# Sharing PSUM banks between two halves of a four-layer vision kernel, and walking its last stage backwards

## The chip, the core and the metric

The kernel runs on one core of a Trainium2 chip. The metric is the device time of one execution in microseconds. Times are the median of several executions; a profile is taken of one further execution, by the hardware profiler.

## The reference

Four layers run one after the other on `x`, eight images of 64 channels by 64 x 64 pixels, in fp32. Cut to what matters here:

```python
# layer 0: attention over all 4096 pixels of an image, depthwise 3x3, 1x1
v = relu(bn(einsum('bchw,oc->bohw', x, w1)))
prob = softmax(einsum('bdn,bdm->bnm', Q, Q) / sqrt(64))        # Q = x as (b, 64, 4096)
out = bn(conv1x1(relu(bn(dwconv3x3(einsum('bnm,bdm->bdn', prob, V)))))) + x
# layer 1: two Swin blocks (8x8 windows, 8 heads, the second shifted by 4)
for i in range(2):
    t = t + window_attention(layernorm(t))
    t = t + gelu(layernorm(t) @ f1w + f1b) @ f2w + f2b
# layer 2: 3x3 filter with weights made from the data, leaky relu, 1x9 convolution, residual
# layer 3: selective scan in four directions, then SAFM
xi, z = split(layernorm(x) @ in_proj)                          # 128 channels each
xc = silu(dwconv3x3(xi))
for k in range(4):                                             # rows, columns, both reversed
    dts, Bs, Cs = split(xproj[k] @ xs[k])
    dt = softplus(dtproj[k] @ dts + dtproj_b)
    h = h * exp(dt * A) + dt * Bs * xs                         # 16 states, along 4096 pixels
    y += sum_over_states(h * Cs) + D * xs
x = x + (layernorm(y) * silu(z)) @ outproj
n = channel_layernorm(x)
out = x + gelu(aggr @ concat(dwconv of 4 groups, pooled by 1, 2, 4, 8, brought back up)) * n
```

## The kernel before

**Tiling.** Two images stand on the 128 partitions at a time, 64 channels each, so the batch is four pairs p = 0 to 3. A pair's 4096 pixels are worked in eight columns of 512 pixels (`CH` and `TD`, one PSUM bank of fp32 each). All of it is in the class `_Direct`. A second, general path at the end of the program runs only when the data are out of range; with these inputs it does not run.

**Stages.** For each pair there are three: `front(p)` (layers 0, 1, 2, and `scan_sources`, which makes xc, its transposed copy and z for the scans and writes them to memory), `scans(p)` and `back(p)`. The front and the back are generators that yield after each piece of work with a number that says how much it was. `tile_kernel` runs `front(0)` alone; then four times `scans(p)`, each with the list `back(p-1)`, `front(p+1)` beside it; then `back(3)` alone. Inside `scans`, after each of its steps, `next(beside, cost)` is drawn until the share of the work done matches the share of the steps gone, over all but the last 24 (`LEAD`). The cost of a back is put at 0.25 of that of a front. Beside the last scans there is only `back(2)`, and with this estimate it is used up about half way, at step 257 of 512; from then on `done >= cost`, and the rest of the last scans runs alone.

**The scans.** A pair has 64 units: two images, four directions, eight chunks of 512 pixels. A unit has eight steps with two of the 16 states each, so 512 steps. `inputs` (L1643 and on) prepares the next unit: SP loads `xs`; PE makes the bank `pdd` (L1655); ACT applies Exp and Ln (L1657, L1660); DVE multiplies into `du` (L1661); PE makes the bank `pbc` (L1664) and ACT copies it to `bc`, which SP writes out as `rows`. A step then takes: SP's two fetches of B and C, each spread over all partitions (L1675); POOL's product `vd` = B x du (L1680); for each of two states ACT's `dad` = exp(du x A) into a bank (L1700), DVE's scan along the 512 pixels (L1703) and ACT's copy of the last value into `carry` (L1711); then the product with C, on POOL for both states (L1714), or, in odd steps and throughout the last pair, one on POOL (L1716) and one on DVE (L1717); and PE adds both products with an identity matrix into the bank `yd` (L1730). At the end of a unit DVE adds `yd` to `Y` (L1741 and around), and in the fourth direction SP writes the sum out as `ys`, which the back reads.

**The front, where banks are used.** `normed` (L1199) is a norm over channels: PE `pc` (L1201, centred values), ACT `n_sq` (L1203), PE `pv` (L1205), ACT `n_sd` by Ln and Exp (L1207, L1208); it leaves `pc` in its bank until DVE has used it. Window attention goes through eight rows of eight windows: scores into `w_s` (PE L1393), bias on DVE (L1405), Exp on ACT (L1410), weighing into `w_av` (PE L1420), division on DVE (L1436), transposing into `w_ot` (PE L1444), and projection into `w_pp`. The multi-layer perceptron (MLP), column by column: `normed`, two `ph` (PE L1485), two Gelus on ACT (L1487), `pf` (PE L1492), and its sum on DVE. `scan_sources`: eight columns of `normed`; then per image eight `pi` (PE) with ACT's copies into the padded tile `XI` (L1570), the 3x3 convolution on DVE over nine taps a column (`xacc`, L1217 and L1221), Silu on ACT (L1577), and eight `pz` with Silu and a write to memory.

**The back.** The first loop takes the columns from 0 to 7. Per column there are three norms: for either image `yb` and `zb` are loaded, `normed` gives `pc` and `pv`, DVE makes `u` (L1765, L1766) and PE multiplies into `po` (L1767); then DVE adds into `X` (L1769), and a third `normed` and DVE write the padded tile `F` (L1772). Then come three pooling levels (L1785 and on), then eight columns of the closing part: nine taps of `sacc` on DVE (L1217, L1221), ACT's copy `S` (L1808), PE `pa` (L1810, L1814), Gelu, and two operations of DVE (L1822 to L1825) before the write.

**Banks.** All eight PSUM banks are given out by two pools. `ps_scan` has three with the tag "da" (`dad`, `pdd`, `pbc`) and one with the tag "y" (`yd`). `ps_front` has three with the tag "f", which all of `bank()` comes from (L1178), and one with the tag "acc", which `total()` gives (`po` of layer 0, `w_av`). A tag's banks go round: the next tile takes the one used longest ago and waits until that one's last reader is done.

**Order.** The instructions are issued in the order of the program, and a scheduler of the framework then sets each engine's order with the waits that buffers and data need. It decides again whenever a pool or a loop changes, so an edit to a pool can move instructions that are not named in it. On the chip the order is fixed.

Of the kernel before, what the change touches and what calls it, by code (L numbers as in the profile page):

```python
# [9 lines left out]
F32 = mybir.dt.float32  # L10
# [5 lines left out]
B, C, HH, WW = 8, 64, 64, 64  # L16
L = HH * WW
P = 128
CH = 512
NCH = L // CH  # L20
# [4 lines left out]
TD = 512  # L25
# [200 lines left out]
class _Net:  # L226
    def __init__(self, ctx, tc, x, packs, layout, out):
        self.tc, self.nc = tc, tc.nc
        self.x, self.out = x, out
        nc = self.nc  # L230
        self.const = ctx.enter_context(tc.tile_pool(name="const", bufs=1))
        self.dram = ctx.enter_context(tc.tile_pool(name="rows", bufs=2, space=bass.MemoryType.DRAM))
        self.packs, self.layout, self.w = packs, layout, {}
        self.load(self.const, (0, 1))
        with tc.tile_pool(name="temp", bufs=1) as temp:
            self.load(temp, (2,))
            self.prepare()
# [910 lines left out]
class _Direct:  # L1148
# [8 lines left out]
    def __init__(self, net, ctx):  # L1157
        self.net, self.tc, self.nc, self.w = net, net.tc, net.nc, net.w
        tc = self.tc
        self.dram = ctx.enter_context(tc.tile_pool(name="mem", bufs=2, space=bass.MemoryType.DRAM))  # L1160
        one = ctx.enter_context(tc.tile_pool(name="scan1", bufs=1))
        self.Y = one.tile([P, L], F32, name="Y", tag="Y")
        self.carries = one.tile([P, NST], F32, name="carry", tag="carry")
        self.sw = ctx.enter_context(tc.tile_pool(name="scan", bufs=2))
        self.slabs = ctx.enter_context(tc.tile_pool(name="slabs", bufs=3))
        self.ps = ctx.enter_context(tc.tile_pool(name="ps_scan", bufs=3, space=PSUM))
        self.pf = ctx.enter_context(tc.tile_pool(name="ps_front", bufs=3, space=PSUM))
        self.kept = {}

    def padded(self, name):  # L1170
        t = self.slabs.tile([P, SLAB], F32, name=name, tag="slab").rearrange("p (h w) -> p h w", w=66)
        self.net.pad_border(t, 66, self.nc.vector)
        return t
# [1 line left out]
    def flat(self, name):  # L1175
        return self.slabs.tile([P, SLAB], F32, name=name, tag="slab")[:, 0:L]

    def bank(self, name, shape=(P, CH)):  # L1178
        return self.pf.tile(list(shape), F32, name=name, tag="f")

    def total(self, name, shape=(P, CH)):
        return self.pf.tile(list(shape), F32, name=name, tag="acc", bufs=1)
# [431 lines left out]
    def scans(self, p, beside, cost):  # L1614

        self.units = []
        for im in range(2):
            out = self.memory("ys")  # L1620
            self.kept["y", 2 * p + im] = out
            for nth, k in enumerate((1, 3, 0, 2)):
                order = range(NTD) if k < 2 else range(NTD - 1, -1, -1)
                self.units += [dict(image=2 * p + im, k=k, c=c, at=at, nth=nth, out=out) for at, c in enumerate(order)]
        self.inputs(self.units[0])
        n = 8 * len(self.units)
        steps = [{} for _ in range(n)]
        done = 0
        for i in range(-3, n):
            if i + 3 < n:  # L1630
                self.fetch(i + 3, steps[i + 3], 0)
            if 0 <= i + 2 < n:
                self.fetch(i + 2, steps[i + 2], 1)
                self.products(i + 2, steps[i + 2])
            if i >= 0:
                self.step(i, steps[i])
                if i:
                    self.sums(i - 1, steps[i - 1], steps[i]["w"])
                while done < cost * (i + 1) / (n - LEAD):
                    done += next(beside, cost)  # L1640
            if i % 8 == 1 and i // 8 + 1 < len(self.units):
                self.inputs(self.units[i // 8 + 1])
        self.sums(n - 1, steps[n - 1])  # L1643
        self.run(beside)
# [37 lines left out]
    def step(self, i, st):  # L1682

        nc, w, net = self.nc, self.w, self.net
        wk, ps = self.sw, self.ps
        u = self.units[i // 8]
        k, c, at, CC, v = u["k"], u["c"], u["at"], st["C"], st["v"]

        n0, rp = 2 * (i % 8), i % 2 or u["image"] >= B - 2
        rev = k >= 2  # L1690

        def along(t):
            return t[:, ::-1] if rev else t

        h = wk.tile([P, 2 - i % 2, TD], F32, name="hd", tag=f"h{i % 2}", bufs=1)
        hs = []
        for j in range(2):
            n = n0 + j
            da = ps.tile([P, TD], F32, name="dad", tag="da")
            nc.scalar.activation(da, u["du"][:, 0], AF.Exp, scale=net.As[:, k, n : n + 1])  # L1700
            first = 0.0 if at == 0 else self.carries[:, n : n + 1]
            to = da if rp and j else h[:, j]
            nc.vector.tensor_tensor_scan(along(to), along(da), along(v[:, j]), first, ALU.mult, ALU.add)  # L1703
            hs.append(to)
            if at < NTD - 1 and (rp or j):
                ends = h[:, :, 0] if rev else h[:, :, TD - 1]
                cs = self.carries[:, n0 : n0 + 2]
                if rp:
                    ends = to[:, 0:1] if rev else to[:, TD - 1 : TD]
                    cs = self.carries[:, n : n + 1]  # L1710
                nc.scalar.activation(cs, ends, AF.Copy)  # L1711

        if rp == 0:
            st["w"] = nc.gpsimd.tensor_tensor(v, h, CC, ALU.mult)  # L1714
        else:
            st["w"] = nc.gpsimd.tensor_tensor(v[:, 0], h[:, 0], CC[:, 0], ALU.mult)  # L1716
            nc.vector.tensor_tensor(v[:, 1], hs[1], CC[:, 1], ALU.mult)  # L1717
# [30 lines left out]
    def back(self, p):  # L1748
# [2 lines left out]
        X = self.flat("X3")  # L1751
        F = self.padded("F")
        with tc.tile_pool(name="w4", bufs=2) as wk:
            for c in range(NCH):
                cols = slice(c * CH, (c + 1) * CH)
                nc.sync.dma_start(X[:, cols], self.kept["x", p][:, cols])
                po = self.bank("po3")
                for im in range(2):
                    y = wk.tile([P, CH], F32, name="yb", tag="yb")
                    z = wk.tile([P, CH], F32, name="zb", tag="zb")  # L1760
                    nc.sync.dma_start(y, self.kept["y", 2 * p + im][:, cols])
                    nc.sync.dma_start(z, self.kept[2 * p + im][2][:, cols])
                    pc, sd = self.normed(wk, lambda pc: [(pc, y)], w["cen128"], w["avg128"], net.eps[:, 0:1])
                    u = wk.tile([P, CH], F32, name="u", tag="u")
                    nc.vector.scalar_tensor_tensor(u, pc, w["on_g"], sd, ALU.mult, ALU.mult)  # L1765
                    nc.vector.scalar_tensor_tensor(u, u, w["on_b"], z, ALU.add, ALU.mult)  # L1766
                    nc.tensor.matmul(po[half[im]], lhsT=w["opT"], rhs=u, start=True, stop=True)  # L1767
                    yield 6
                nc.vector.scalar_tensor_tensor(X[:, cols], po, w["outproj_b"], X[:, cols], ALU.add, ALU.add)  # L1769
                pc, sd = self.normed(wk, lambda pc: [(pc, X[:, cols])], w["cen64"], w["avg64"], net.eps[:, 1:2])  # L1770
                d = self.rows(F, c)
                nc.vector.scalar_tensor_tensor(d, self.img(pc), w["cn_g"], self.img(sd), ALU.mult, ALU.mult)  # L1772
                nc.scalar.activation(d, d, AF.Identity, bias=w["cn_b"])
                yield 6
# [55 lines left out]
@with_exitstack  # L1830
def tile_kernel(ctx: ExitStack, tc: tile.TileContext, x: bass.AP, packs, layout, out: bass.AP):
    net = _Net(ctx, tc, x, packs, layout, out)
    with ExitStack() as path:
        net.open(path, True)
        d = _Direct(net, path)
        net.log_exp()
        front = d.run(d.front(0))
        back = 0.25 * front
        for p in range(B // 2):
            works, cost = [], 0  # L1840
            if p:
                works.append(d.back(p - 1))
                cost += back
            if p + 1 < B // 2:
                works.append(d.front(p + 1))
                cost += front
            d.scans(p, d.chain(*works), cost)
        d.run(d.back(B // 2 - 1))

    with tc.tile_pool(name="check", bufs=1) as pool:  # L1850
        bad = net.in_range(pool)
    with tc.If(bad > 0), ExitStack() as path:
        net.open(path, False)
        for p in range(B // 2):
            t = net.layer0(p)
            t = net.layer1(t)
            t = net.layer2(t)
            net.layer3(t, p)
# [21 lines left out]
```

## Time and profile before

| | |
|---|---|
| median of 3 runs | 14083.28 us (14071.26 to 14084.42) |
| the profiled execution, its own time | 14074.21 us |
| its span, first to last instruction | 14072.3 us |
| mean granted clock of TensorE | 0.865 |

The page's first part gives each engine's busy time over the span; the groups give the costliest kinds of instructions (busy time and mean duration, then idle time just before them and what ended most of it):

```profile
PE 11340.1 (81%) x46358; PEld 4189.8 (30%) x46358; DVE 8432.1 (60%) x9763; ACT 7036.3 (50%) x15453; POOL 8173.2 (58%) x4111
...
L1680 POOL TENSOR_TENSOR vd<-B,du 128x1024 f32<-128x1024 f32 x2048 | 4842.5, 2369 | 3955.8 <-DVE xacc L1217 1888.8
L1730 PE MATMUL yd<-vd,pack 128*128 128x512 f32 x8192 | 4577.0, 686 | 1175.1 <-POOL vd L1714 419.8
L1703 DVE TENSOR_TENSOR_SCAN hd<-dad,carry,vd 128x512 f32<-128x512 f32 x2464 | 3092.6, 1270 | 1081.7 <-ACT dad L1700 681.2
...
L1716 POOL TENSOR_TENSOR vd<-hd,C 128x512 f32<-128x512 f32 x1280 | 1634.9, 1278 | 271.7 <-DVE hd L1703 244.6
```

The stages differ in what fills them. The windows of the trace give the busy time of each engine in each stage, here rounded to whole microseconds; the stage's borders are read from the timeline.

| stage (us from the span's start) | length | PE | DVE | ACT | POOL | clock |
|---|---|---|---|---|---|---|
| front 0: attention, 0 to 600 | 600 | 580 | 11 | 334 | 2 | 1.00 |
| depthwise and 1x1, to 670 | 70 | 23 | 65 | 12 | 0 | 0.57 |
| first norm, to 704 | 34 | 24 | 7 | 22 | 0 | 0.80 |
| window rows, block 0, to 985 | 281 | 238 | 72 | 91 | 0 | 0.61 |
| MLP, block 0, to 1070 | 85 | 57 | 11 | 43 | 0 | 0.60 |
| window rows, block 1, to 1355 | 285 | 241 | 83 | 92 | 0 | 0.64 |
| MLP, block 1, to 1452 | 97 | 64 | 13 | 51 | 0 | 0.62 |
| layer 2, to 1792 | 340 | 315 | 78 | 33 | 0 | 0.70 |
| scan sources and first inputs, to 1977 | 185 | 89 | 110 | 84 | 20 | 0.61 |
| scans of pairs 0 to 2 with their works, to 11650 | 9673 | 8139 | 6048 | 5173 | 6285 | 0.89 |
| last scans with back 2, to 12812 | 1162 | 770 | 1003 | 578 | 970 | 0.88 |
| last scans alone, to 13785 | 973 | 644 | 811 | 460 | 897 | 0.90 |
| last back, to 14072 | 287 | 156 | 119 | 65 | 0 | 0.61 |

A row is read against its length: an engine that is busy for nearly all of it sets the stage's time; where none is, the stage is a chain of dependent steps on several engines.

### The profile page before, as it was taken

To read this page: it belongs to the slowest core of one execution; us is meant where nothing else is said; L and a number is where in the kernel's file an instruction comes from. 1 tells how busy PE (TensorE), PEld (TensorE's weight loads), DVE (VectorE), ACT (ScalarE), POOL (GpSimd) and SP (SyncE) were. 2 spreads that over 40 slices of the span, in tenths; PEclk is the share of its full clock that TensorE was granted. 3 is DMA by queue.
4 is the path that set the end of the run, shared out by engine and by line. 5 is a ranking of instruction groups with operands and counts; after the bars stand their busy time and mean duration, and the time that the engine had idled before them with its cause. 6 is when DMAs were issued, how large, how long until landed. Compare 5 with 4: busy or idle time off the path is not lost. (4 is left out here: it accounts for less than half of the span.)

```text
span 14072.3 us, 141532 instructions
## 1 busy us (share of the span) xinstructions
PE 11340.1 (81%) x46358; PEld 4189.8 (30%) x46358; DVE 8432.1 (60%) x9763; ACT 7036.3 (50%) x15453; POOL 8173.2 (58%) x4111
## 2 busy tenths in 40 slices
PE   9888879979889668998889666998988866666665
PEld 2244222224433222223433222222443222222221
DVE  0222254467776875347675767336666677998884
ACT  5533145555553645555562644555554454454442
POOL 0000035677776765456674685456666678879991
PEclk9866679989889889998898788999888878988996
DMA  0000034456555764345553675345554577878882
GB/s 17 1 1 1 5 136 153 161 187 211 195 196 181 241 206 156 127 147 181 175 197 133 225 247 180 128 144 175 170 173 168 181 244 256 276 241 291 294 291 70
DMA packets 705498, 2379.22 MB, mean 169 GB/s; under 512 B 81060, under 2 KB 81188, under 8 KB 703980
## 3 DMA queue, kind: packets, MB, share of 16 engines
q1 hardware_dynamic: 681024, 2315.57, 48.5%
q10 hardware_dynamic: 23724, 54.50, 1.0%
q8 instruction: 367, 6.01, 0.2%
q14 instruction: 383, 3.14, 0.1%
HBM read 2269.08 MB, written 100.66 MB: 168 GB/s over the span
## 5 line engine op out<-in xcount | busy, mean ns | idle before, releaser
L1680 POOL TENSOR_TENSOR vd<-B,du 128x1024 f32<-128x1024 f32 x2048 | 4842.5, 2369 | 3955.8 <-DVE xacc L1217 1888.8
L1730 PE MATMUL yd<-vd,pack 128*128 128x512 f32 x8192 | 4577.0, 686 | 1175.1 <-POOL vd L1714 419.8
L1703 DVE TENSOR_TENSOR_SCAN hd<-dad,carry,vd 128x512 f32<-128x512 f32 x2464 | 3092.6, 1270 | 1081.7 <-ACT dad L1700 681.2
L1700 ACT ACTIVATE dad<-du,As 128x512 f32<-128x512 f32 x4096 | 2711.7, 679 | 985.0 <-DVE hd L1703 728.8
L1730 PEld LDWEIGHTS yd<-vd,pack 128*128 128x128 f32 x8192 | 1592.5, 212 | 3853.7 <-issue 1753.0
L1714 POOL TENSOR_TENSOR vd<-hd,C 128x1024 f32<-128x1024 f32 x768 | 1810.9, 2358 | 1365.4 <-DVE hd L1703 694.1
L1716 POOL TENSOR_TENSOR vd<-hd,C 128x512 f32<-128x512 f32 x1280 | 1634.9, 1278 | 271.7 <-DVE hd L1703 244.6
L1272 ACT ACTIVATE e<-s 128x512 f32<-128x512 f32 x2048 | 1199.2, 591 | 1030.0 <-PE s L1266 1028.1
L1703 DVE TENSOR_TENSOR_SCAN dad<-dad,carry,vd 128x512 f32<-128x512 f32 x1120 | 1426.0, 1273 | 62.7 <-ACT dad L1700 62.5
L1266 PE MATMUL s<-X 64*128 64x512 f32 x4096 | 1350.1, 646 | 114.1 <-ACT e L1272 113.8
L1258 PE MATMUL po<-e,VT 128*64 128x512 f32 x4096 | 1145.1, 629 | 17.0 <-ACT e L1272 17.0
L1711 ACT ACTIVATE carry<-hd 128x1 f32<-128x1 f32 (+1 forms) x1792 | 357.1, 201 | 1172.7 <-DVE hd L1703 1161.9
L1717 DVE TENSOR_TENSOR vd<-dad,C 128x512 f32<-128x512 f32 x1280 | 858.7, 671 | 82.1 <-ACT carry L1711 74.8
L1266 PEld LDWEIGHTS s<-X 64*128 64x128 f32 x4096 | 365.3, 186 | 1065.4 <-issue 820.8
L1420 PEld LDWEIGHTS w_av<-vals,w_e 64*64 64x64 f32 x16384 | 612.7, 159 | 178.0 <-ACT w_e L1410 69.9
L1420 PE MATMUL w_av<-vals,w_e 64*64 64x9 f32 x16384 | 638.5, 216 | 23.6 <-ACT w_e L1410 23.5
L1703 DVE TENSOR_TENSOR_SCAN hd<-dad,vd 128x512 f32<-128x512 f32 x352 | 420.2, 1210 | 203.0 <-ACT dad L1700 92.0
L1741 DVE TENSOR_TENSOR Y<-Y,yd 128x512 f32<-128x512 f32 x128 | 124.6, 973 | 656.0 <-PE yd L1730 655.7
L1410 ACT ACTIVATE w_e<-w_e 128x512 f32<-128x512 f32 x512 | 310.4, 627 | 382.2 <-DVE w_e L1405 254.9
L1655 PE MATMUL pdd<-xs,xdt 128*128 128x512 f32 x512 | 323.4, 718 | 204.3 <-DVE hd L1703 96.7
L1711 ACT ACTIVATE carry<-dad 128x1 f32<-128x1 f32 x1120 | 189.9, 170 | 589.1 <-DVE dad L1703 587.0
L1405 DVE TENSOR_TENSOR w_e<-w_s,bias 128x512 f32<-128x512 f32 x512 | 328.5, 682 | 248.4 <-PE w_s L1393 248.1
(247 smaller groups left out, 11078.1 us busy)
## 6 DMA issues: line engine op xcount, KB each, us to landing
B<-rows SPq DMA_DIRECT2D x2048, 512.0 KB, 5.0
C<-rows SPq DMA_DIRECT2D x2048, 512.0 KB, 4.5
xs<-xt SPq DMA_DIRECT2D x128, 256.0 KB, 2.9
xs<-xc SPq DMA_DIRECT2D x128, 256.0 KB, 3.1
xc<-xcv ACTq DMA_DIRECT2D x64, 256.0 KB, 4.3
zs<-z ACTq DMA_DIRECT2D x64, 256.0 KB, 3.9
xt<-XT ACTq DMA_DIRECT2D x32, 512.0 KB, 7.5
rows<-bc SPq DMA_DIRECT2D x256, 64.0 KB, 1.9
```

What stands on the lines that cost most here:

```text
L1258: nc.tensor.matmul(po[half[im]], lhsT=VT[:, t, half[im]], rhs=es[im], start=(t == 0), stop=(t == 31))
L1266: nc.tensor.matmul(ss[im], lhsT=at(half[im], t), rhs=X[half[im], jc * CH : (jc + 1) * CH], start=True, stop=True)
L1272: nc.scalar.activation(e, ss[im], AF.Exp, scale=C**-0.5, accum_out=parts[:, im, t, jc : jc + 1])
L1420: nc.tensor.matmul(self.av[half[im], x % 4 + j, h, :], lhsT=es[h // 4][half[im], j, h % 4, :], rhs=V[half[im], x + j, h, :], start=True, s ...
L1680: self.nc.gpsimd.tensor_tensor(v, st["B"], dx.to_broadcast([P, 2, TD]), ALU.mult)
L1700: nc.scalar.activation(da, u["du"][:, 0], AF.Exp, scale=net.As[:, k, n : n + 1])
L1703: nc.vector.tensor_tensor_scan(along(to), along(da), along(v[:, j]), first, ALU.mult, ALU.add)
L1711: nc.scalar.activation(cs, ends, AF.Copy)
L1714: st["w"] = nc.gpsimd.tensor_tensor(v, h, CC, ALU.mult)
L1716: st["w"] = nc.gpsimd.tensor_tensor(v[:, 0], h[:, 0], CC[:, 0], ALU.mult)
L1717: nc.vector.tensor_tensor(v[:, 1], hs[1], CC[:, 1], ALU.mult)
L1730: m = nc.tensor.matmul(y, lhsT=w["ident"], rhs=st["v"][:, j], start=(n == 0), stop=(n == NST - 1))
```

## The change

It has three parts. First, a counter `self.turn` is kept; while it is at or above zero, each call of `bank()` takes its tile from the tags "f" and "da" in turn, so that six banks go round instead of three. It is on during the whole of `front(0)`, off after it, and on again from the point in the last scans at which their beside work is used up, through to the end, so also in the last back. Second, the scans take `dad` by `bank()` with "da" as the default; while the counter is off that is the pool they had, and while it is on `dad` too alternates. `pdd` and `pbc` stay in "da" throughout, `yd` in "y". Third, the first loop of `back` goes through the columns from the last to the first, in all four backs; the closing loop keeps its order.

```diff
@@ __init__
+        self.turn = -1
@@ bank
-    def bank(self, name, shape=(P, CH)):
-        return self.pf.tile(list(shape), F32, name=name, tag="f")
+    def bank(self, name, shape=(P, CH), ours="f"):
+
+        if self.turn >= 0:
+            self.turn += 1
+            ours = ("f", "da")[self.turn % 2]
+        return (self.pf if ours == "f" else self.ps).tile(list(shape), F32, name=name, tag=ours)
@@ scans
                 if i:
                     self.sums(i - 1, steps[i - 1], steps[i]["w"])
+                if p == B // 2 - 1 and done >= cost:
+                    self.turn = max(self.turn, 0)
                 while done < cost * (i + 1) / (n - LEAD):
@@ step
-            da = ps.tile([P, TD], F32, name="dad", tag="da")
+            da = self.bank("dad", (P, TD), "da")
@@ back
-            for c in range(NCH):
+            for c in reversed(range(NCH)):
                 cols = slice(c * CH, (c + 1) * CH)
@@ tile_kernel
         net.log_exp()
+        d.turn = 0
         front = d.run(d.front(0))
+        d.turn = -1
         back = 0.25 * front
```

## The prediction

> **What bounds the kernel now.** I read the page first, then the busy time of the engines in short windows, then the timeline wherever a stage that the change touches begins, repeats or ends, and last the chain of waits. The change can act in three places: the first front, which runs alone; the second half of the last scans; the last back, which runs alone again. The scans between them keep their pools.
>
> ```profile
> span 14072.3 us, 141532 instructions
> ...
> PE   9888879979889668998889666998988866666665
> ...
> POOL 0000035677776765456674685456666678879991
> ```
>
> A slice is 352 us. PE's 9, 8, 8, 8, 8 over POOL's zeros are the first front (to about 1955 us), POOL's nines the last scans, its final 1 the last back. The windows say what holds each:
>
> ```profile
> 550.00:600.00 50.00, 50.00 (x194) 12.05 (x192) 0.69 (x1) 30.41 (x96) 0.00 (x0) 1.00 0.00 1
> 600.00:650.00 50.00, 17.98 (x139) 9.48 (x138) 47.23 (x70) 7.78 (x10) 0.00 (x0) 0.60 0.00 0
> 1000.00:1050.00 50.00, 34.27 (x57) 8.47 (x57) 6.02 (x9) 25.65 (x32) 0.00 (x0) 0.64 0.00 0
> 13400.00:13500.00 100.00, 64.76 (x123) 21.21 (x122) 87.78 (x90) 50.28 (x127) 97.58 (x56) 0.95 0.89 301
> ```
>
> The columns are PE, weight loads, DVE, ACT, POOL, granted clock, DMA share, GB/s. To 600 us PE is full: more banks give nothing. From 600 DVE is full with the convolution: nothing either. At 1000 (the MLP) nobody is full: a chain of PE, ACT and DVE. In the last scans POOL works 97 of 100 us. The timeline shows the chains, first one row of windows, then one MLP column:
>
> ```profile
> 732.75 1.03 PE L1444 MATMUL w_ot<-pack,w_o 128*64 128x128 f32 x4 [1.02 <-DVE w_o L1436]
> ...
> 736.18 2.07 PE L1205 MATMUL pv<-n_sq,pack 128*128 128x512 f32 x2 [0.69 <-ACT n_sq L1203]
> ```
> ```profile
> 1011.87 1.26 ACT L1487 ACTIVATE hid<-ph,bf 128x512 f32<-128x512 f32 x2 [0.76 <-PE ph L1485]
> 1012.61 2.55 PE L1492 MATMUL pf<-hid,pack 128*64 128x512 f32 x4 [0.74 <-ACT hid L1487]
> 1013.15 1.28 ACT L428 ACT_TABLE_LOAD   x1
> 1015.09 1.66 PE L1201 MATMUL pc<-X,pack 128*128 128x512 f32 x2
> ...
> 1017.43 1.12 PE L1205 MATMUL pv<-n_sq,pack 128*128 128x512 f32 x2 [0.69 <-ACT n_sq L1203]
> ```
> ```profile
> 1870.00 0.11 DVE L411 MEMSET XI<- 128x64 f32 x1
> 1897.37 0.69 DVE L1661 TENSOR_TENSOR du<-pdd,xs 128x512 f32<-128x512 f32 x1 [27.26 <-ACT pdd L1660]
> 1900.30 0.81 DVE L1221 TENSOR_SCALAR xacc<-XI,pack 128x512 f32<-128x512 f32 x1 [2.24 <-ACT XI L1570]
> ```
>
> The last fence is DVE idle for 30 us before the second image's convolution. For the end, the chain of waits gives the period of one column of the back, 13887.48 - 13863.49 = 24.0 us:
>
> ```profile
> 13863.49 2.02 PE pc L1201 x2
> 13866.18 2.09 PE pv L1205 x2
> ...
> 13887.48 2.02 PE pc L1201 x2
> ```
>
> **What the Trainium skill says.** "PSUM — Partial Sum Buffer", Specifications: eight banks of 512 fp32 values in each partition. The pools hold 3 + 1 and 3 + 1, all eight; so nothing is added, the change only lets one side use the other's three while that side rests. "TensorE: Matmul & The Clock Gate", Part 1: the clock is halved after about 3.4 us of idling and full after about that much steady work. The trace agrees: a pair of 128x512 passes takes 2.09 us in the chain above and 1.12 us at 1017. The same page, Architectural detail: ACT and DVE take their instructions strictly in order, so one placed early that is not ready holds all behind it; below, ACT's second XI waits 4.63 us for pi with pdd behind it. "ScalarE: Activation LUTs", What ACT_TABLE_LOAD costs: 1283 ns a load, and 1.28 us is what the trace has.
>
> **The change part by part.** The framework orders each engine's instructions anew, so I compared the built order of both programs. Outside the three places it differs only around the backs beside the scans; no compute instruction is added, and ACT gets 7 more table loads.
>
> First front. (a) Rows of windows: PE now takes half of the next scores before the first transpose, filling its 1.0 us wait for DVE, and the next row's pc inside the weighing, so that n_sq is done when pv comes: 0.69 us. 1.7 us x 15 rows = 25. (b) MLP: pc of the next column stands before pf. Before, pv came 1017.43 - 1011.87 = 5.6 us after the Gelus began (6.0 at half clock). After: pc 0 to 2.1, pf to 4.1 at half clock, while ACT does Gelus, load and n_sq by 1.26 + 1.28 + 0.60 = 3.2; pv at 3.3 to 4.1. Say 2.0 x 15 columns = 30. (c) First norm: it took 30 us for 8 columns; ACT needs 0.58 + 0.69 + 0.63 + 0.72 = 2.62 each, 21, so 8; the norm of the sources 3.05 to 2.62, 3; p_m ahead of the last pf, 2. (d) Second image: all eight pi now stand before the scans' pdd, which had held PE 7.05 us for a DMA and left ACT waiting 4.63 us for pi. ACT's first XI stays at 1885.3, its second comes at once, so the convolution starts near 1887, 13 earlier, and without two of the scans (1.2 each): 16. Sum 84. Bounds: 50 (the filled holes return half to PE's slower matmuls) and 110.
>
> The price of (d): the first scan's pdd moves behind that convolution; its wait is taken from the first steps. Behind it on ACT stand two xcv, then loads for Silu, Ln, Silu and Exp in turn (three loads more, 3.9 us). From the end of the convolution: xcv and XT 2.8, four DMA issues 3, z and load 2, Ln 0.6, z and two loads with its issue 3.6, du and bc 1.2, then 5.9 as before from bc to POOL's first product, 2 x 2.35 for two more: step 2's scan at about +26. Before, it began at 1977.2, 25.8 after the convolution. So zero, within 10 either way.
>
> Last scans, from step 257 of 512: the last 260 steps took 973 us, 3.74 each; POOL needs 2.373 + 1.275 = 3.65. The floor is thus 24 us away. More banks let dad run ahead at unit borders, where DVE sat 83 us over 23 borders waiting for du; but SP's fetches keep their place. I take 10; bounds 25 gained, and 15 lost.
>
> Backs beside the scans: reversed columns no longer wait for the last unit's ys (PE stood 58.6 us in 16 waits for yb, matmuls and weight loads together, the last back's included). Four loads more at half-busy ACT are hidden. I take 5, bounds 25 either way, since DVE is 90 to 99 per cent busy in the third of them and any bad order shows.
>
> Last back. Its early start does not come: in the built order a single pc (yb) is ahead of the last yd, and before, the first image's po was already done in the scans; the first column needs about 20 us against 21. Per column the order becomes pc pc pv po pv po pc pv. At half clock throughout: eight pairs 16.4 + gaps 3.0 + 3.0 + 0.92 + 0.67 + 0.6 (n_sq before Exp) = 24.6, no gain; if the second pc and first pv come at full clock, as five pairs now follow without a gap, 22.3. Between +4 and -12 for seven columns; I take -8. Reversal also puts the first four sacc taps behind the last column instead of in DVE's idle time: 4 x 0.75 = +3, memsets moved out -1; the closing columns, DVE 59 of 66 us busy, -3. Together -9.
>
> Sum: 84 + 10 + 5 + 9 = 108. The profiled execution took 14074.2 us (span 14072.3): 13966. The median, 14083.3, is 9 above that execution: 13975.
>
> **The rivals.** *The clock takes it back.* The front's windows already grant 0.6; if work put in the holes runs at half speed, (a) and (b) vanish, as do last scans and back: 29 + 5 remain, 14049. For: PE 43 of 50 us busy in the rows. Against: pc in the MLP replaces waiting, not matmuls. *A larger gain.* Denser rows lift the clock from about 0.62 to 0.8: of 560 us of rows some 400 hang on PE, a fifth is 80 to 90 more: 13888. For: the same matmuls take 1.12 us elsewhere; against: no row shows it. *Slower: the head of POOL's queue.* In the last half POOL's order moves in most units; if at each border a product waits for its B while a ready vd stands behind it, the steps fall to the 4.2 to 4.4 us of the half with the back beside it. At 0.55 more for 255 steps: +140 - 108, 14115. It decides from (108 + 28) / 255 = 0.53 us a step. For: POOL waited 29.5 us for B already there. Against: the pattern at a border, three products, one vd, two products, then vds, is the same in both orders. *The change does not do what it says*: for the reversal's head start this is so, and it is in the sum.
>
> **How the numbers follow.** A measurement here tells 0.2 per cent, 28 us, from no change. Forecast 0.62 (own range 13930 to 14030), clock 0.16, larger gain 0.14, slower 0.08. The range 13900 to 14052 holds the forecast, most of the clock case and part of the larger gain. Faster: 0.61 + 0.09 + 0.14 = 0.84; same 0.09; slower 0.07.
>
> **What would show it.** The second image's convolution ending near 1867 instead of 1951 us, and POOL's first product 19 later, near 1886 instead of 1904.87; the convolution's first xacc of image two within 3 us of the second XI; MLP columns near 8 to 10 us; rows near 33; steps of 3.65 to 3.75 in the last half; column period 22 to 24.6 at the end. The forecast is wrong if the front's end moves by less than 50 us, or if the last half takes more than 3.85 us a step.

## The result, and the profile after

| | before | changed |
|---|---|---|
| median, runs taken side by side | 14077.27 us (14064.28 to 14084.42) | 14018.69 us (14012.53 to 14040.87) |
| ratio, with its 95% interval | | 0.9962 (0.9945 to 0.998) |
| span of the profiled execution | 14072.3 us | 14010.7 us |

The kernel became faster, by 58.6 us; 108 were forecast. On the page of the changed kernel POOL's first slice of work, the sixth, has a 4 instead of a 3: the scans begin earlier.

```profile
span 14010.7 us, 141613 instructions
...
POOL 0000046578767765556665685457666688878982
```

The same four windows as before (PE, weight loads, DVE, ACT, POOL, granted clock, DMA share, GB/s) show where to look:

```profile
550.00:600.00 50.00, 49.76 (x234) 14.07 (x234) 3.60 (x10) 28.07 (x90) 0.00 (x0) 1.00 0.00 1
600.00:650.00 50.00, 17.30 (x92) 7.71 (x88) 48.69 (x75) 8.99 (x12) 0.00 (x0) 0.58 0.00 0
1000.00:1050.00 50.00, 35.79 (x207) 13.59 (x206) 10.74 (x15) 31.91 (x41) 0.00 (x0) 0.83 0.00 0
13400.00:13500.00 100.00, 62.55 (x113) 21.86 (x114) 83.12 (x87) 44.46 (x99) 93.99 (x54) 0.90 0.87 289
```

In the MLP at 1000 us ACT is busier and the clock is 0.83 where it was 0.64. In the last scans POOL, which had been busy for 97.58 of 100 us, is at 93.99. POOL is what those scans wait for, so they must have become slower. To say by how much, I took one event that all kernels have in the same number, the end of the addition of `yd` into `Y` at the end of each of the 256 units, and compared it between the two traces. Units are counted from 0 in each pair's scans, and the lead is the time by which the changed kernel is earlier:

| place | before | changed | lead |
|---|---|---|---|
| end of the second image's convolution | 1951.5 | 1863.9 | 87.6 |
| end of unit 1 of the first scans | 2064.5 | 1983.9 | 80.6 |
| end of the scans of pair 0 | 4981.1 | 4916.0 | 65.1 |
| pair 1 | 8338.9 | 8258.6 | 80.3 |
| pair 2 | 11691.4 | 11612.9 | 78.5 |
| unit 31 of the last scans | 12806.8 | 12720.2 | 86.6 |
| unit 63, the last | 13785.7 | 13760.3 | 25.4 |
| end of the span | 14072.3 | 14010.7 | 61.6 |

Three things happened. The front gained 88 us. The second half of the last scans lost 61 of them. The last back gained 36. In between, the lead wanders by up to 15 us, also over the scans of pair 0, whose code is unchanged.

**The front.** Here is one MLP column of the changed kernel in the timeline (start, duration, engine, line; the lines of the changed kernel are 5 to 7 higher, so L1201 is now L1206 and L1680 is L1687):

```profile
998.54 2.01 PE L1206 MATMUL pc<-X,pack 128*128 128x512 f32 x2
998.64 1.26 ACT L1492 ACTIVATE hid<-ph,bf 128x512 f32<-128x512 f32 x2 [1.46 <-PE ph L1490]
...
1000.48 1.08 PE L1497 MATMUL pf<-hid,pack 128*64 128x512 f32 x4
...
1001.86 1.12 PE L1210 MATMUL pv<-n_sq,pack 128*128 128x512 f32 x2 [0.31 <-ACT n_sq L1208]
```

The next column's `pc` now runs beside the Gelus, ahead of `pf`, and `pv` comes 3.2 us after the Gelus begin; it was 5.6. `pf` takes 1.08 us here, where it took 2.55 in the column shown before; over the columns of both blocks it is 1.5 us in the mean, where it was 2.5. `pv` takes 1.12 us in this column and took 1.12 in that one; its mean goes from 1.5 to 1.2. From the first `ph` of a block to the last it is 59.5 and 59.2 us in the two blocks, before it was 82.1 and 80.2.

DVE at the second image's convolution:

```profile
1805.99 0.11 DVE L411 MEMSET XI<- 128x64 f32 x1
1815.92 1.53 DVE L1226 TENSOR_SCALAR xacc<-XI,pack 128x512 f32<-128x512 f32 x2 [9.82 <-ACT XI L1575]
```

Its idle time is 9.8 us where it was 30.

**The last scans.** What POOL waited for between the ends of units 32 and 59, first before, then changed (us in total, times, longest):

```profile
POOL vd L1716 <- DVE hd L1703: 26.5, 28, 1.7
POOL vd L1680 <- DMA B<-rows: 24.8, 16, 3.0
```
```profile
POOL vd L1723 <- issue: 44.9, 17, 2.9
POOL vd L1687 <- DMA B<-rows: 30.0, 29, 1.7
POOL vd L1723 <- DMA C<-rows: 22.4, 16, 2.0
```

Units 33 to 40 now take 33.5 to 35.4 us each, and from unit 41 on short units of 27.6 us and long ones of 35 take turns; before, most of these units took 28 to 33. The timeline of POOL and DVE around the border of a long one:

```profile
13374.27 2.35 POOL L1687 TENSOR_TENSOR vd<-B,du 128x1024 f32<-128x1024 f32 x1 [0.29 <-DMA B<-rows]
13379.24 1.27 POOL L1723 TENSOR_TENSOR vd<-hd,C 128x512 f32<-128x512 f32 x1 [2.63 <-issue]
...
13390.41 1.27 POOL L1723 TENSOR_TENSOR vd<-hd,C 128x512 f32<-128x512 f32 x1 [1.39 <-DMA C<-rows]
13393.06 2.35 POOL L1687 TENSOR_TENSOR vd<-B,du 128x1024 f32<-128x1024 f32 x1 [1.39 <-DMA B<-rows]
```
```profile
13371.71 1.29 DVE L1710 TENSOR_TENSOR_SCAN dad<-dad,carry,vd 128x512 f32<-128x512 f32 x1 [1.63 <-POOL vd L1687]
...
13374.01 1.29 DVE L1710 TENSOR_TENSOR_SCAN dad<-dad,carry,vd 128x512 f32<-128x512 f32 x1 [0.43 <-POOL vd L1687]
...
13376.65 1.29 DVE L1710 TENSOR_TENSOR_SCAN dad<-dad,carry,vd 128x512 f32<-128x512 f32 x1 [0.76 <-POOL vd L1687]
13377.85 1.26 DVE L1710 TENSOR_TENSOR_SCAN hd<-dad,carry,vd 128x512 f32<-128x512 f32 x1
```

A scan that writes `hd` is the first of a step's two states, one that writes `dad` in place is the second. DVE runs the second states of four steps before the first state of the first of them (one stands just ahead of these lines). Before, first and second states take turns at every border, as here:

```profile
13396.26 1.28 DVE L1703 TENSOR_TENSOR_SCAN hd<-dad,carry,vd 128x512 f32<-128x512 f32 x1 [0.44 <-ACT dad L1700]
13397.46 1.27 DVE L1703 TENSOR_TENSOR_SCAN dad<-dad,carry,vd 128x512 f32<-128x512 f32 x1
13398.64 1.26 DVE L1703 TENSOR_TENSOR_SCAN hd<-dad,carry,vd 128x512 f32<-128x512 f32 x1
```

Over the whole stretch, DVE's turned order stands in units 33 to 40 and in every second one from 42 on, and these are the long units; the short ones have the order of before. At the border shown, the `hd` scan ends at 13379.11, and POOL's product with it starts at 13379.24: the 2.63 us that the profile calls "issue" are POOL standing at the head of its queue before a product whose scan DVE does late. There are 17 such waits, and 17 of the 27 units have the turned order. Then the fetches, whose buffers come free late in turn, are late too.

**The last back.** The chain of waits over one column of the changed kernel:

```profile
13852.37 2.09 PE pc L1206 x2
...
13855.13 2.07 PE pv L1210 x2
13857.20 2.35 PE pc L1206 x4
13859.56 0.97 PE pv L1210 x2
...
13863.87 1.07 PE po L1774 x2
13864.94 1.75 PE pv L1210 x2
...
13869.69 1.98 PE po L1774 x2
...
13872.50 2.09 PE pc L1206 x2
```

A column takes 20.1 us here, 20.3 in the mean; before, 24.0. Both images' `pc` follow each other without a gap and take 2.35 us together, where one alone took 2.02 us in the chain before. The clock granted over these columns is 0.69; it was 0.56.

### The profile page after: what moved, and what is told of

It is laid out like the page before. It is cut to its first block, busy times and chain, and to the rows that moved or that the text cites. A ratio compares the mean times of both kernels' runs of the same rounds, so it can differ in the third digit from the quotient of the medians.

```text
span 14010.7 us, 141613 instructions
## 1 busy us (share of the span) xinstructions
PE 11364.2 (81%) x46358; PEld 4240.7 (30%) x46358; DVE 8425.0 (60%) x9763; ACT 7041.2 (50%) x15460; POOL 8178.9 (58%) x4111
## 5 line engine op out<-in xcount | busy, mean ns | idle before, releaser
L1687 POOL TENSOR_TENSOR vd<-B,du 128x1024 f32<-128x1024 f32 x2048 | 4841.8, 2369 | 3920.1 <-DMA B<-rows 2103.0
L1737 PE MATMUL yd<-vd,pack 128*128 128x512 f32 x8192 | 4625.9, 695 | 1265.4 <-POOL vd L1721 449.5
L1737 PEld LDWEIGHTS yd<-vd,pack 128*128 128x128 f32 x8192 | 1624.1, 215 | 3956.6 <-issue 1863.1
L1263 PEld LDWEIGHTS po<-e,VT 128*64 128x64 f32 x4096 | 212.9, 136 | 824.6 <-issue 581.0
```

The lines of the kernel that those rows point to most:

```text
L1263: nc.tensor.matmul(po[half[im]], lhsT=VT[:, t, half[im]], rhs=es[im], start=(t == 0), stop=(t == 31))
L1687: self.nc.gpsimd.tensor_tensor(v, st["B"], dx.to_broadcast([P, 2, TD]), ALU.mult)
L1737: m = nc.tensor.matmul(y, lhsT=w["ident"], rhs=st["v"][:, j], start=(n == 0), stop=(n == NST - 1))
```

## The experiments

All are timed in five rounds beside the kernel before, on one chip for each group of four. The kernel before took 14077.97 us beside the first four runs, 14060.05 beside swap, no_scans, late_turn and inputs_f, and 14077.56 beside the last four. A difference across groups is thus uncertain by some 17 us, and the times of a step from the profiles are the safer comparison there. "Last half" is the time of a step between the ends of units 32 and 63 of the last scans, "back" the time from the last unit's end to the end of the span, both from the run's own profile. Before, they are 3.800 us and 286.6 us; in the changed kernel 4.074 and 250.4.

### The parts alone

**front_only** has the change's first part alone:

```diff
+        d.turn = 0
         front = d.run(d.front(0))
+        d.turn = -1
```

> Only the first front alternates; last scans, last back and the direction of the back are as before. Theory A (the parts add up): the front gains about 87 us by the end of the second image's convolution (1951.5 to about 1864), the first product of POOL comes near 1888, the first unit ends 80 us earlier and the lead is kept: 13995 to 14005 us against 14080. Rival (the lead is lost in the scans, as it shrank from 82 to 65 us over pair 0 in the changed kernel): about 14015 to 14020.

Measured 13994.96 us (ratio 0.994, 0.9927 to 0.9953), 83 us less than before. The convolution ends at 1867.0, POOL's first product is at 1890.9, the lead at unit 1 is 77.2 us; it is 55.5 at the last unit in the profiled execution, the slowest of the five, as the rival has it, but the median of the five keeps it. For the median theory A stands; the single executions, from 13975.58 to 14017.08 us, cover both.

**scans_only** alternates in the last half of the last scans and sets the counter back to -1 ahead of the last back:

```diff
+                if p == B // 2 - 1 and done >= cost:
+                    self.turn = max(self.turn, 0)
...
+        d.turn = -1
         d.run(d.back(B // 2 - 1))
```

> Only the dad tiles of the last half of the last scans alternate; nothing else does. Theory A: the loss of about 62 us between unit 32 and unit 63 of the last scans belongs to this part alone: POOL waits for a product whose scan stands late in DVE's order, 3.98 us a step instead of 3.74, and the time is 14140 us against 14080. Rival (it is the new state in which the scans find themselves: another clock, another phase after a reversed back 2): no more than 20 us lost.

Measured 14139.69 us (1.0049, 1.0036 to 1.0062): 62 us more than before. Last half 4.062. At unit 31 of the last scans it stands 1.0 us behind before, at unit 63 66.1. The loss belongs to this part alone.

**reverse_only** has the reversed loop and nothing else:

```diff
-            for c in range(NCH):
+            for c in reversed(range(NCH)):
```

> Only the columns of the back's first loop are reversed. Theory A: the backs beside the scans gain about 12, 7 and 14 us, since their first columns no longer wait for the last unit's sums; the last back gains the head start (its first column does not need the last unit), about 5 us, and keeps 24.0 us a column: 14040 to 14050 us. Rival (the order inside the last back's columns comes from the direction, not from the banks): a column near 20 us and 14020 us or less.

Measured 14009.33 us (0.9956, 0.9943 to 0.9969), 69 us less. A column still takes 24.0 us, so the rival falls, but theory A had the sizes wrong by far: the last back takes 233.9 us, 53 less. The backs beside the scans give about 12 us between unit 1 and the last unit, not 33; another 12 stand at unit 1 already, in code that the edit does not touch. `X` of the first two columns is written 119 and 19 us before the last unit's end. Two of eight columns run inside the scans.

**backalt_only** alternates in the last back alone, columns from the first on:

```diff
+        d.turn = 0
         d.run(d.back(B // 2 - 1))
```

> Only the last back alternates, with the columns from the first to the last. Theory A: more banks let the second image's pc and pv run before the first's are done, so a column takes 20 to 21 us instead of 24.0 and the closing columns 58 instead of 64: 14045 to 14055 us. Rival (only the direction matters): within 5 us of before.

Measured 14045.54 us (0.9975, 0.9963 to 0.9988), 32 us less; 20.3 us a column, back 251.2. As theory A has it.

Alone, reversal and alternation take 53 and 35 us from the back. The changed kernel, which has both, has only 36 off, and its first `X` begins 9.4 us after the last unit: the head start is gone.

### Why the parts don't add up, and what the last scans wait for

**swap** is the changed kernel with the counter started at 1 in the last scans, so that `hd` takes "f" and the second states share "da" with `pdd` and `pbc`.

```diff
-                    self.turn = max(self.turn, 0)
+                    self.turn = max(self.turn, 1)
```

> The changed kernel with the parity of the alternation turned round in the last scans: the first state's dad (hd) takes "f", the second's, which is kept in its bank until the product with C, shares "da" with the inputs' pdd and pbc. Theory A (it is the order: with hd's banks held by the inputs, DVE runs four second states first and POOL, in order, stands before a product with C whose scan is late): now the first states run ahead, POOL's order has no product that waits, a step of the last half takes 3.7 instead of 4.07 us, about 90 us less: near 13930 us. Rival (six banks in the round cost time by themselves, by clock or by contention): as the changed kernel, 14005 to 14030 us.

Measured 14038.71 us (0.9978, 0.9969 to 0.9986); last half 4.107. The order did turn round (up to three first states ahead of their second ones, in every unit from 33 on), and POOL's wait for a late scan went from 45 us of "issue" to 12 us put down to `hd`, but 57 us of waits for C and 45 for B took their place. The time is close to the rival's and a little above it, yet the waits are of another kind: something else stands in the way.

**no_scans** is the changed kernel without the alternation in the last scans; the counter is set to 0 just before the last back:

```diff
-                if p == B // 2 - 1 and done >= cost:
-                    self.turn = max(self.turn, 0)
...
+        d.turn = 0
         d.run(d.back(B // 2 - 1))
```

> The changed kernel with the alternation off in the last scans; it is on in the first front and, from its first column, in the last back. Theory A (a tile of "da" asked for by the back stands behind the last dad in that tag's round, so the back's head start over the scans is lost when its first columns alternate): last half 3.80 us a step, back about 250 us from the last sum as in the changed kernel, not 234 as with the reversal alone: 13945 to 13955 us. Rival (the head start was lost because dad took "f"): back about 205 us, 13900 to 13910 us.

Measured 13966.7 us (0.9925, 0.9912 to 0.9938); last half 3.801, back 254.2. The loss of the scans is gone, the head start has not come back: only the first column's `pc` of either image runs early, and the first `X` begins 12.8 us after the last unit. So it isn't dad's taking of "f" that loses it. A back's tile of the tag "da" is asked for after the last `dad`, so in that tag's round it would wait for the scans to end; the next run tests this.

**late_turn** lets columns 7 and 6, which come first, take "f" alone.

```diff
             for c in reversed(range(NCH)):
                 cols = slice(c * CH, (c + 1) * CH)
+                if p == B // 2 - 1 and c == 5:
+                    self.turn = 0
```

> As no_scans, but the last back alternates only from its third column on (the reversed loop's columns 7 and 6 take "f" alone). Theory A: two columns run inside the scans as with the reversal alone (53 us), and the other columns take 20.3 instead of 24.0 us: back about 210 us, 13905 to 13915 us. Rival (head start and short columns don't add up): 234 us or more, 13930 us or more.

Measured 13916.54 us (0.9889, 0.9872 to 0.9905); back 213.5, with `X` of the first columns 115 and 19 us before the last unit's end. Head start and short columns add up once the early columns stay out of the scans' banks.

**inputs_f** adds to it, for steps 257 to 472 of the last scans (`self.late`, set where the counter was set), `pdd` and `pbc` from "f":

```diff
-        pd = ps.tile([P, TD], F32, name="pdd", tag="da")
+        pd = self.pf.tile([P, TD], F32, name="pdd", tag="f") if self.late else ps.tile([P, TD], F32, name="pdd", tag="da")
```

and the same for `pbc`.

> As late_turn, and from step 257 to 472 of the last scans pdd and pbc come from "f", so that dad has "da" for itself. Theory A (at unit borders dad and the inputs compete for three banks, and DVE waits for du): DVE's order at a border is the same as inside a unit, and a step takes 3.68 us over those 27 units instead of 3.80, about 25 us less: near 13885 us. Rival (the border waits for the load of xs or for B's and C's fetches, not for a bank): within 8 us of late_turn.

Measured 13989.43 us (0.9944, 0.9932 to 0.9956), 73 us more than late_turn. Last half 4.044, which is 62 of the 73. Another 15 are in the last back, which takes 228.1 us: only one column, not two, now runs ahead of the last unit's end. That this comes from sharing "f" with `pdd` and `pbc` up to step 472 is likely, but was not tried. For the steps neither theory holds, and the run is telling, because DVE's order is just what was wanted: first and second states take turns in every unit. SP's queue in the timeline shows why:

```profile
13309.35 0.32 SPq L1682 DMA_DIRECT2D B<-rows  x1
13317.97 0.32 SPq L1675 DMA_DIRECT2D rows<-bc  x1
13318.39 0.36 SPq L1682 DMA_DIRECT2D C<-rows  x1
13318.84 0.40 SPq L1682 DMA_DIRECT2D B<-rows  x1
```

SP issues nothing for 8.3 us: the write of `rows` stands at its head and waits for ACT's `bc`, and the fetches of C and B stand behind it. Then they all leave at once. In 26 of 27 units this gap is over 4 us (218 us over all 27; before, 74). In swap it is 7.1 us in nearly every unit, 195 in all. In the changed kernel it is 0.1; there SP waits at a fetch of C instead, up to 7.6 us, for the buffer that the late product holds.

**inputs_f_act** takes that write out of SP's queue:

```diff
-        nc.sync.dma_start(rows, bc)
+        (nc.scalar if self.late else nc.sync).dma_start(rows, bc)
```

> As inputs_f, but while pdd and pbc come from "f" ACT issues the write of rows, which SP issued before. Theory A2 (with more banks the inputs' place moves away from where ACT can serve it, and SP, in order, stands 8.3 us at the write of rows until bc is there, with the fetches of C and B behind it): without that write in SP's queue the fetches run on, POOL's waits for B and C go from 112 us over 27 units to under 25, and a step takes 3.68 instead of 4.04 us: about 85 us less than inputs_f, near 13895 us. Rival (six banks cost time by themselves, by a lower clock or by contention): 4.0 us a step, 13975 to 14000 us.

Measured 13881.55 us (0.986, 0.9844 to 0.9877), 108 us less than inputs_f, which ran in another group; last half 3.617, 0.43 us a step less, which is 106 us over the 248 steps. Against late_turn, 3.794, banks and write together bring 44 us over these steps, and the last back, 231.4 us here as well, gives 18 of them back. POOL's waits over the 27 units, first inputs_f, then inputs_f_act:

```profile
POOL vd L1723 <- DMA C<-rows: 73.9, 26, 4.0
POOL vd L1687 <- DMA B<-rows: 38.0, 31, 2.7
POOL vd L1723 <- DVE hd L1710: 2.5, 2, 1.4
```
```profile
POOL vd L1687 <- DMA B<-rows: 6.1, 8, 2.7
POOL vd L1723 <- DVE hd L1710: 4.2, 3, 1.7
```

112 us of waiting for fetches became 6, and POOL works nearly without a break. The rival (more banks cost time by themselves, by a lower clock) falls: the granted clock in this stretch was 0.82 in inputs_f and is 0.90 here, with the same banks, so the lower clock went with the waiting and did not cause it.

**late_turn_act** is late_turn with the same line, `pdd` and `pbc` left in "da".

> As late_turn (pdd and pbc in "da"), with ACT issuing the write of rows from step 257 of the last scans on. Theory A2: SP's waits for bc were 66 us over 27 units there, of which POOL felt about 20: 3.72 instead of 3.79 us a step, 13890 to 13905 us. Rival (the three banks at the border are what holds DVE): 3.79 us a step, 13910 to 13920 us.

Measured 13926.26 us (0.99, 0.9882 to 0.9918); last half 3.833. Nothing gained, as the rival says: a step is not shorter than in late_turn. With three banks for `dad`, `pdd` and `pbc` together, POOL's waits are for `hd` (26.5 us) and B (24 us), as in late_turn. It takes both, the banks of their own and the write out of SP's way.

### The rows of windows, and the write in all scans

**no_row_turn** is inputs_f_act with the counter at -1 from the first window head of a block to its last row:

```diff
+                on = self.turn >= 0
+                self.turn = -1 if on else self.turn
                 now = self.window_head(i, 0, X, wk)
...
+                self.turn = 0 if on else self.turn
                 yield from self.mlp(i, X, wk)
```

> As inputs_f_act, with the alternation off in the rows of windows of the first front and on in the rest of it. Theory A (in the rows PE's holes are filled, and its matmuls then take longer, so that nothing is gained): the rows take 233 and 237 us from the first to the last w_pp of a block instead of 235 and 244, and the whole 0 to 10 us less than inputs_f_act. Rival (the filled holes are worth 1.7 us a row): the rows take 25 us more than with the alternation.

Measured 13864.02 us (0.985, 0.9833 to 0.9866). That is 18 us less than inputs_f_act, more than forecast. The rows take 228.6 and 235.4 us, in inputs_f_act 232.9 and 242.6; the rest of the 18 is not accounted for. Over all the profiles, eight with the alternation in the rows and six without, the means are 235.2 and 244.2 against 231.7 and 237.0: the alternation costs some 11 us over both blocks. The windows of before and of front_only over 200 us of rows of the first block:

```profile
750.00:950.00 200.00, 168.65 (x2164) 109.88 (x2163) 51.41 (x110) 63.80 (x102) 0.00 (x0) 0.61 0.01 1
```
```profile
737.00:937.00 200.00, 179.57 (x2160) 118.47 (x2160) 51.02 (x110) 62.32 (x101) 0.00 (x0) 0.59 0.01 1
```

PE does about the same number of matmuls and is busy for 11 us more; the clock is no higher. Over the whole first block of front_only PE's idle time before `w_ot` falls from 16.3 to 7.4 us, as one of two waits in each row goes, and before `pv` from 5.5 to nothing. But the same 512 `w_s` take 60.1 us instead of 49.3 and the same 2048 `w_av` 102.8 instead of 94.6. What filling the holes gives is paid back in slower matmuls.

**rows_act_all** has ACT issue the write of `rows` in all four scans:

```diff
-        (nc.scalar if self.late else nc.sync).dma_start(rows, bc)
+        nc.scalar.dma_start(rows, bc)
```

> As no_row_turn, with ACT issuing the write of rows in all four scans. Theory A: SP's waits at rows are 390 to 430 us a pair in the scans with works beside, but POOL waits for fetches only some 60 us a pair there, as PE's backlog ends last; at most 30 us less than no_row_turn over three pairs, and if ACT's issue delays dad, up to 20 us more. Rival (SP's waits at rows hold these scans too): 100 us or more less.

Measured 13934.28 us (0.9901, 0.9885 to 0.9918), 70 us more than no_row_turn. The lead over before shrinks from 82 us at unit 1 to 20 at the end of pair 2, while in no_row_turn it is 87 and 85 there. It is worse than either theory allowed for. ACT carries the front's work in its queue there besides `dad`, and the order of the engines is another again. Through these three pairs POOL's waits for fetches of B stay as they were (154 and 161 us), so the move freed nothing there; its waits for late `hd` scans grow from about 810 to 900 us. Which of the two changes brings that was not tried and stays open.

## Why the prediction was right or wrong

The time lay in the range and on the forecast side, but that is luck in good part: it is the sum of one term that was right in size and two wrong ones of opposite sign, and inside the right one, too, errors cancel.

- *First front, 84.* Measured 87.6 at the end of the convolution, and made up otherwise than I said. A single execution is loose here: by the means of four profiles without the alternation and eight with it throughout the front, the convolution ends at 1944.7 and 1864.0 us, which is 81. In its parts:
  - The rows: 25 forecast; they gave 2 in this execution by one block and cost 3 by the other, and over all profiles cost 11. For the rows alone the first rival, "the clock takes it back", has the outcome: the matmuls became slower, though the granted clock hardly moved (0.61 and 0.59 in the windows shown). The 3.4 us of idling that the prediction quotes for a halved clock do not account for a clock near 0.6 there: no hole of PE in either window is longer than 2.4 us.
  - The MLP: 30 forecast, 43.6 measured. `pv` came 3.2 us after the Gelus began, about as forecast; the rest fits the shorter `pf`, 1.0 us a column. A higher clock from denser work is what the rival of the larger gain supposed, for the rows; it came in the MLP alone, 0.64 to 0.83. (ACT's 1.26 + 1.28 + 0.60 in the forecast make 3.1, not 3.2; nothing hangs on it.)
  - The first norm: 8 forecast, 9.2 measured from the first `cacc` to the first `w_s`, which takes in the convolution ahead of it; of that, 3.8 fall after its last tap.
  - The second convolution: 16 forecast, 23.8 measured from the first `pi`.
  - Layer 2 with the norm of the sources and `p_m`: 5 forecast, 6.3 measured. The start of the kernel gave 4.6 that I had at nothing.
- *Start of the scans, 0 within 10.* From the convolution's end to unit 1, 7 us were lost. POOL's first product came 17.2 us earlier, where 19 follow from the forecast; it stands 23.8 us behind the end of the convolution, not 19.
- *Last scans, 10 gained, bounds 25 and 15 lost.* Measured 61 lost, from 3.80 to 4.07 us a step. **This is the step that failed.** It took more banks to let `dad` run ahead at the borders, and put a changed order of DVE at nothing. The rival "the head of POOL's queue" named the place and the kind of wait, and I gave it 0.08, with the argument that POOL's own pattern at a border is the same in both orders. But the order of DVE, which makes what POOL waits for, had changed at every border of units 33 to 40 and at every second one after that, and I had not read it there. So POOL's largest wait is for a late scan (44.9 us), not for B as the rival had it; waits for B and C come behind (30.0 and 22.4 us). The size was half of the rival's: 0.27 us a step, below its own turning point of 0.53. The bound that I had set for the forecast itself, 3.85 us a step, was passed. The starting point was off as well: I divided the last 973 us by 260 steps, but POOL makes only 254 products with C in them, so a step took 3.8 us, not 3.74, and POOL's floor of 3.65 was some 45 us away, not 24. The 10 us that I took stay under either.
- *Backs beside the scans, 5 within 25.* From unit 1 of the first scans to unit 31 of the last the lead goes from 80.6 to 86.6 us, so 6. The runs cannot tell this from their own wandering: three kernels with the front code of before ended unit 1 earlier than it by 2.6, 11.7 and 13.2 us.
- *Last back, 9.* Measured 36.2. That the head start doesn't come was right for this kernel, and the runs give the reason: with the alternation in the back's first columns it can't. What was mis-sized is the term "eight pairs 16.4" of the column. In the chain above PE's eight pairs take 2.09 + 2.07 + 2.35 + 0.97 + 1.07 + 1.75 + 1.98 = 12.3 us, where I had 16.4: four of them take 1.0 to 1.2 us and one 1.75, not 2.05. The rest of the column, 7.9 us, is about what I had (8.2). I had allowed for two pairs at the short time (22.3 us). Over seven columns that is 27 us instead of 8. The first `X` ends 10.1 us after the last unit instead of 15.4, so 5 more, where I had seen 1. From the last column's `X` to the last sum of the output it takes 92.5 us instead of 96.6, where I had 1 less.

So the front, the last back and the last scans make 87.6 - 7 + 6 - 61 + 36 = 62 us, the difference of the spans.

A version with the front's alternation outside the rows, reversal, alternation from the third column of the last back, and the inputs' own banks with the write of `rows` on ACT in the last half (no_row_turn) takes 13864.02 us, 1.5 per cent less than before, while the changed kernel is 0.4 per cent less.

## What to carry to other kernels

Giving a stage more buffers is also an edit of every engine's order: before pricing it, read the order of each engine at the stage's borders, the producer's as well as the one of the engine that waits, and the DMA queue's. An instruction placed early and not ready held all that was behind it here, on POOL for 2.6 us and in SP's queue for 8.3. If two streams share a round of buffers, the later one in program order does not get ahead of the earlier one; what is to have a head start needs buffers that the other does not take. Where a change pays in one stage and costs in another, as here, try it without the stage that has an engine full.

## What was not expected of the hardware

SP's wait before one small write, 8.3 us in nearly each unit ahead of 64 KB of `rows`, was worth 0.43 us in each step, 106 us over the second half of the last scans. The banks had made that wait so long (it was 2.8 us in most units before), and without them taking the write out of SP's queue brought nothing. And filling PE's idle holes gave opposite results in two places: in the MLP the matmuls around became faster (`pf` from 2.5 to 1.5 us in the mean, clock 0.64 to 0.83), while in the rows of windows PE's busy time rose from 168.65 to 179.57 us in 200 and the clock stayed near 0.6. What decides between the two was not measured.
